# Four interleaved stages after an attention: later key-value products, own orders for the last periods, regrouped activations

## The chip, the cores and the metric

One Trainium2 chip, one core of it. The metric is the device time of one execution in microseconds (us), of which three runs are given and their median is taken. The engines are called PE (matrix products; PEld is its weight load), DVE (vector engine), ACT (scalar engine, for activation functions), POOL (GpSimd) and SP (the engine that issues most transfers).

## The reference, cut to what matters

The input is 4 x 2048 rows of 256 channels. Four sub-layers follow one another, each of the form `x = x + layernorm(sublayer(layernorm(x)))`:

```python
x = x + _layernorm(_L0_attn_ref(_layernorm(x), ...))  # softmax attention, 16 heads of 16
x = x + _layernorm(_L0_ffn_ref(_layernorm(x), ...))   # "f"
x = x + _layernorm(_L1_attn_ref(_layernorm(x), ...))  # "a" and "b"
x = x + _layernorm(_L1_ffn_ref(_layernorm(x), ...))   # "i"

# f: mix every row with the one before it, then
r = sigmoid(xr @ W_r.T); k = relu(xk @ W_k.T) ** 2; out = r * (k @ W_v.T)
# a, b: z = layernorm(x, g1, be1); Q = elu(z @ wq.T) + 1; K = elu(z @ wk.T) + 1; v = z @ wv.T
KV = einsum('nshd,nshv->nhdv', K, v / length)         # over a whole batch of 2048 rows
x = x + Q·KV / (Q·sum(K));  x = x + gelu(layernorm(x, g2, be2) @ w1.T + b1) @ w2.T + b2
# i: weights are integers times 1/127
out = (silu(x @ wg.T) * (x @ wu.T)) @ wd.T
```

Everything is float32.

## The kernel before, in words

The softmax attention comes first (up to about 3,100 us of the span) and writes its result to DRAM tiles `mid`. It is not touched by the change. After it, `rest` treats the other three sub-layers in 16 blocks of 512 rows (four tiles of 128 rows), four blocks to a batch. `narrow` is a flag computed on the chip from the weights; in this execution it is 1, so stage i splits its left operands into a rounded part (`hT`, `gT`) and a remainder (`hL`, `gL`) and makes two fast products of each.

The work of a block is cut into four stages, written as Python generators that yield after each named part:

- `stage_f` (line 155): sums, norm, turn (transposes of `h`, evacuated by ACT into `hT`), mix (ACT scales into `shift`, DVE multiplies and adds into `xk`, `xr`), k0, k1, r, v, osums (statistics of the output on DVE, power on POOL), x (`apply` on DVE, residual on POOL, store to `mid`).
- `stage_a` (line 219): sums, norm, norm2, turn, q0, q1, kv0 to kv3, kv4. Each kv part multiplies one tile for keys and values (one PSUM tile, 128x512), applies `elu1` (DVE minimum, ACT exponential, DVE maximum and sum) to get `K`, and copies the values to `V` on ACT. `gather` then accumulates K^T V into two PSUM tiles over a batch. Part kv_i gathers tile i-1, and kv4 gathers tile 3; in the last block of a batch kv4 also copies the result to `kvm` (16 small DVE copies).
- `stage_b` (line 282): pre (POOL writes the normalised x to `hb`, line 287), msg (Q times `kvm`, DVE divides, POOL adds to `hb`, line 310), sums, norm, turn, up0 to up3 (eight products with GELU on ACT into `hf`), down0 to down3 (DVE adds the bias, POOL adds `hb`, line 332), osums, x.
- `stage_i` (line 341): sums, norm, turn, gate0 to gate5, down0 to down3, osums, x (with the store to `out`). A gate part makes two PSUM tiles; ACT takes SiLU of the first (`gs`), DVE multiplies by the second, ACT rounds to `gT`, POOL makes `gL` (line 382).

A loop over periods p (line 436) steps through these parts in an order written out as a string. In period p, f works on block p, a on block p-2, b on block p-6 and i on block p-7. `next:` and `last:` in the string mean the generator of the following or the preceding period. The order `RAMP` (line 416) serves p = 0 to 5, `FULL` (line 409) all later periods. Since there are 16 blocks, f ends with p = 15, a with p = 17, b with p = 21, i with p = 22 (its last two parts with p = 23).

PE, ACT and DVE instructions of `rest` stay in program order (class `InOrder`, line 38; that is why the profile gives line 46 for nearly all of them). POOL and SP instructions are placed by the scheduler. All matrix products of `rest` share four rotating PSUM tiles `m` (`mm_tile`, line 96), all transposes two tiles `t`; a product waits until the reader of the tile four allocations earlier is done. `hb` has one buffer, `K` two, `V` two (`vs`, line 91), `msg` three, `QT` five.

Of the kernel before, what the change touches and what calls it, by code (L numbers as in the profile page):

```python
# [10 lines left out]
FP = mybir.dt.float32  # L11
# [7 lines left out]
P = 128  # L19
C = 256  # L20
CC = C // P
# [28 lines left out]
def rest(ctx: ExitStack, tc: tile.TileContext, a: dict, out_rows, mids, env: dict, narrow: bool):  # L50
    nc = tc.nc
# [16 lines left out]
    NB = B * NBLK  # L68
    LAG_A, LAG_B, LAG_I = 2, 2 + NBLK, 3 + NBLK
    early = ctx.enter_context(tc.tile_pool(name="early", bufs=3))  # L70
    late = ctx.enter_context(tc.tile_pool(name="late", bufs=3))
    quer = ctx.enter_context(tc.tile_pool(name="quer", bufs=LAG_B - LAG_A + 1))
    small = ctx.enter_context(tc.tile_pool(name="small", bufs=LAG_B - LAG_A + 2))
# [12 lines left out]
    kvms, vs = [], []  # L86
    for r in range(2):
        kvm = one.tile([P, CC, P + 4], FP, tag=f"kvm{r}", name=f"kvm{r}")
        nc.gpsimd.memset(kvm, 0.0)
        kvms.append(kvm)  # L90

        v = one.tile([P, CC, P + 4], FP, tag=f"v{r}", name=f"v{r}")
        nc.gpsimd.memset(v, 1.0 / T)
        vs.append(v)
# [124 lines left out]
    def stage_a(j):  # L219
# [31 lines left out]

        last = None
        for i in range(4):
            kvp = mm_tile()
            linear(kvp, lambda c: zT[:, c, i * P : (i + 1) * P], lambda c: wkv[:, c, :], CC)
            K = two.tile([P, C], FP, tag="K", name="K")
            elu1(K, kvp[:, :C], C)
            V = vs[i % 2]
            act.activation(
                V[:, :, :P],  # L260
                kvp[:, C:].rearrange("p (c d) -> p c d", c=CC),
                AF.Copy,
                scale=1.0 / T,
            )
            if last:
                gather(*last)
            last = i, K, V
            yield f"kv{i}"
        gather(*last)
        if k == NBLK - 1:  # L270
# [11 lines left out]
    def stage_b(j):  # L282
        x, kvm, QT = xs[j], kvms[j // NBLK % 2], queries.pop(j)
        mv, rs = before.pop(j)
        hb = one.tile([P, 4, C], FP, tag="hb", name="hb")
        for i in range(4):
            ln_apply(hb[:, i, :], x[:, i, :], mv, rs, i, nc.gpsimd)
        yield "pre"
        for i in range(4):
# [12 lines left out]
            dve.reciprocal(zr, zr)  # L302
            msg = three.tile([P, C], FP, tag="msg", name="msg")
            dve.tensor_tensor(
# [36 lines left out]
    def stage_i(j):  # L341
# [65 lines left out]


    FULL = (
        "f:turn i:turn b:msg i:gate0 a:turn last:i.osums f:mix i:gate1 b:sums last:i.x load i:gate2 f:k0 "  # L410
# [4 lines left out]
    )  # L415
    RAMP = (
        "load f:turn a:turn f:mix a:q0 next:a.sums a:q1 f:k0 next:a.norm f:k1 a:kv0 next:f.sums a:kv1 "
        "next:a.norm2 a:kv2 next:f.norm a:kv3 f:r a:kv4 f:v f:osums f:x next:b.pre"
    )
# [549 lines left out]
```

## Time and profile before

| | us |
|---|---|
| median of 3 runs | 4578.01 (4574.43 to 4578.36) |
| the profiled execution | 4576.01 |
| its span (first to last instruction) | 4574.2 |
| `rest`, about 3100 to 4574 of the span | 1474 |
| one full period (p = 8 to 15), one is 3592.62 to 3674.50 | 81.88 |
| first i:turn of p = 18 (4272.51) to the end | 301.7 |
| ACT_TABLE_LOAD, 102 of them | 130.9 busy, 1283 ns each |

The span is given in us from its start. In the profile an instruction row has its start, its length, the engine, the line, what it writes and reads, and in brackets the idle time of the engine before it with the instruction that ended that idle time.

### The profile page before, as it was taken

The page shows a single profiled execution, that of the slowest core. Times are in us where ns is not written, and L with a number is a line of the kernel's source. Part 1 is how long each engine was busy: PE and PEld are TensorE (multiplying, and loading weights), DVE is VectorE, ACT ScalarE, POOL GpSimd, SP SyncE. Part 2 cuts the span into 40 slices and gives each one's busy share as a digit, 9 for nine tenths or more (in the row PEclk, how much of TensorE's full clock was granted, in tenths as well). Part 3 has the DMA queues.
Part 4 walks back from the last instruction along what each step waited for, and adds up shares of the span by engine and source line. Part 5 has one row for each costly group of instructions (what it writes and reads, how often), then busy time and mean ns, then how long its engine had stood idle before and what let it go on. Part 6 is the DMA issues. An engine that isn't in the chain of part 4 may idle for free.

```text
span 4574.2 us, 69494 instructions
## 1 busy us (share of the span) xinstructions
PE 4196.7 (92%) x26369; PEld 2196.9 (48%) x26369; DVE 3394.8 (74%) x6847; ACT 2874.5 (63%) x3558; POOL 1089.5 (24%) x1541
## 2 busy tenths in 40 slices
PE   4999999999999999999999999984789899899887
PEld 1444444444444444444444444432456666666665
DVE  4898898988889988889898888954555545554333
ACT  0677777777777777777777777763555555655343
POOL 3100111211001221011121100013234544444344
PEclk9999999999999999999999999997999999999998
DMA  3101101011010020110101101002000000000000
GB/s 107 38 10 29 29 10 42 29 43 36 11 30 23 25 65 10 29 29 10 43 29 31 38 10 29 1 24 72 33 14 28 19 33 24 28 19 19 10 19 15
DMA packets 84568, 130.58 MB, mean 29 GB/s; under 512 B 21376, under 2 KB 41984, under 8 KB 84224
## 3 DMA queue, kind: packets, MB, share of 16 engines
q1 hardware_dynamic: 77920, 122.23, 9.0%
q8 instruction: 210, 3.44, 0.3%
q10 hardware_dynamic: 6304, 3.81, 0.3%
q14 instruction: 134, 1.10, 0.1%
HBM read 33.70 MB, written 25.17 MB: 13 GB/s over the span
## 4 chain that ended last, share of the span: by engine, by line
PE 60%; DVE 21%; ACT 9%; POOL 5%; issue 4%; SPq 1%; DMA 1%; ACTq 0%; POOLq 0%; DVEq 0%
PE acc L46 19%; PE s L46 17%; PE w L46 13%; DVE mx L46 10%; PE m L46 8%; PE t L46 2%; ACT p L46 2%; DVE o L46 2%; ACT h L46 2%; POOL hb L537 2%; ACT L46 1%; DVE gs L46 1%; SPq L662 1%; ACT elu L46 1%; PE ot L46 1%
## 5 line engine op out<-in xcount | busy, mean ns | idle before, releaser
L46 DVE TENSOR_REDUCE mx<-s 128x1 f32<-128x512 f32 x4096 | 2538.8, 682 | 305.0 <-PE s L46 304.9
L46 ACT ACTIVATE p<-w 128x1024 f32<-128x1024 f32 x2048 | 2002.7, 1022 | 824.4 <-PE s L46 556.9
L46 PE MATMUL s<-k,q 64*128 64x512 f32 x4096 | 1664.3, 450 | 56.8 <-DMA k<-lo 30.3
L46 PE MATMUL w<-mrow,pick 64*128 64x512 f32 x4096 | 1406.2, 417 | 0.0
L46 PE MATMUL w<-q,k 64*128 64x512 f32 x4096 | 1369.3, 419 | 0.0
L46 PEld LDWEIGHTS s<-k,q 64*128 64x128 f32 x4096 | 758.5, 186 | 1269.2 <-DVE mx L46 1147.0
L46 PE MATMUL acc<-p,xp 128*32 128x512 f32 x8192 | 1093.3, 605 | 0.0
L46 PEld LDWEIGHTS w<-mrow,pick 64*128 64x128 f32 x4096 | 749.1, 185 | 55.2
L46 PEld LDWEIGHTS w<-q,k 64*128 64x128 f32 x4096 | 670.5, 185 | 58.2 <-ACT p L46 21.7
L627 POOL TENSOR_SCALAR xd<-x,lnx_nm,lnx_rs 128x128 f32<-128x128 f32 x256 | 110.9, 448 | 991.3 <-PE t L46 991.0
L609 POOL TENSOR_SCALAR xp<-x,lnx_nm,lnx_rs 128x64 f32<-128x64 f32 x256 | 99.1, 394 | 921.9 <-PE acc L46 921.0
L46 PEld LDWEIGHTS acc<-p,xp 128*32 128x32 f32 x8192 | 161.6, 108 | 247.0 <-issue 245.8
L46 DVE SCALAR_TENSOR_TENSOR gs<-m,gs 128x512 f32<-128x512 f32 x96 | 66.2, 690 | 226.9 <-ACT gs L46 205.6
L46 PE MATMUL m<-zT,w1T 128*128 128x512 f32 x512 | 225.4, 593 | 0.4 <-ACT zT L46 0.4
L46 PE MATMUL m<-w2T,hf 128*128 128x256 f32 x1024 | 225.6, 379 | 0.0
L46 PEld LDWEIGHTS m<-w2T,hf 128*128 128x128 f32 x1024 | 194.6, 190 | 38.4 <-issue 13.4
L382 POOL TENSOR_TENSOR gL<-gs,gT 128x512 fp32r<-128x512 f32 x96 | 124.4, 1296 | 198.3 <-ACT gT L46 198.2
L46 PE MATMUL t<-ident,h 128*128 128x128 f32 x512 | 90.2, 312 | 88.5 <-ACT h L46 55.9
L46 ACT ACTIVATE elu<-elu 128x256 f32<-128x256 f32 (+1 forms) x96 | 46.7, 487 | 196.4 <-DVE elu L46 196.2
L46 ACT ACT_TABLE_LOAD x102 | 130.9, 1283 | 58.3 <-DVE elu L46 24.6
L46 PEld LDWEIGHTS m<-zT,w1T 128*128 128x128 f32 x512 | 97.4, 190 | 110.6 <-issue 99.3
L140 POOL TENSOR_TENSOR x<-x,o 128x256 f32<-128x256 f32 x192 | 141.8, 767 | 17.9 <-DVE o L46 17.9
(146 smaller groups left out, 4065.4 us busy)
## 6 DMA issues: line engine op xcount, KB each, us to landing
q<-hi SPq DMA_DIRECT2D x256, 64.0 KB, 2.1
k<-hi SPq DMA_DIRECT2D x256, 64.0 KB, 2.1
q<-lo SPq DMA_DIRECT2D x256, 64.0 KB, 2.1
k<-lo SPq DMA_DIRECT2D x256, 64.0 KB, 2.1
mid<-x SPq DMA_DIRECT2D x32, 512.0 KB, 2.6
x<-mid SPq DMA_DIRECT2D x32, 512.0 KB, 3.3
x<-in_x SPq DMA_DIRECT2D x16, 512.0 KB, 5.8
out<-x SPq DMA_DIRECT2D x16, 512.0 KB, 2.9
```

The costliest lines, as they stand in the source:

```text
L46: return lambda *args, **kw: self._tc.keep_in_program_order(method(*args, **kw))
L140: nc.gpsimd.tensor_tensor(x[:, i, :], x[:, i, :], o[:, i, :], ALU.add)
L382: nc.gpsimd.tensor_tensor(gL[:, f, :], gs, gT.bitcast(FP)[:, f, :], ALU.subtract)
L537: dve.tensor_scalar(dst, src, mv[:, i, 0:1], rs[:, i : i + 1], ALU.subtract, ALU.mult)
L609: nc.gpsimd.tensor_scalar(heads(n)[:, i, :, :HD], xs[b][:, i, g * GH * HD : (g + 1) * GH * HD].rearrange("p (h d) -> p h d", d=HD), nm[:, ...
L627: nc.gpsimd.tensor_scalar(xd[:, i], xh.unsqueeze(1).broadcast_to([P, 2, GH * HD]), nm[:, it : it + 1], rs[:, it : it + 1], ALU.add, ALU.mult,)
L662: nc.sync.dma_start(out=dst.bitcast(FP)[r::4, cols], in_=part.bitcast(FP)[c0 : c0 + 32, :])
```

## The change

Gathers come two tiles behind their kv part instead of one, so `K` and `V` get three buffers, and kv4 (now two gathers, and the `kvm` copies) is called in the next period, after f:turn. `hb` gets a second buffer; `msg` and `QT` give one up each. In `FULL`, mix and gate1 come ahead of `last:i.osums`, and all six gate parts come ahead of b:turn (before, gate4 and gate5 were between parts of up). In `RAMP` both q parts come together, the k parts are put between kv parts, and r comes ahead of `next:f.norm`. Two new orders are added: `TURN` for p = 18 and `LATE` for p = 19 to 23. They put i's gates behind b's down, and call the next block's b:msg, b:sums, b:norm and i:turn between and behind them. In the program of the narrow branch the ACT table loads go from 101 to 62 (one more is in the attention).

```diff
-    quer = ctx.enter_context(tc.tile_pool(name="quer", bufs=LAG_B - LAG_A + 1))
+    quer = ctx.enter_context(tc.tile_pool(name="quer", bufs=LAG_B - LAG_A))
...
-    for r in range(2):
-        kvm = one.tile([P, CC, P + 4], FP, tag=f"kvm{r}", name=f"kvm{r}")
-        nc.gpsimd.memset(kvm, 0.0)
-        kvms.append(kvm)
+    for r in range(3):
+        if r < 2:
+            kvm = one.tile([P, CC, P + 4], FP, tag=f"kvm{r}", name=f"kvm{r}")
+            nc.gpsimd.memset(kvm, 0.0)
+            kvms.append(kvm)
...
-        last = None
+        behind = []
         for i in range(4):
             kvp = mm_tile()
             linear(kvp, lambda c: zT[:, c, i * P : (i + 1) * P], lambda c: wkv[:, c, :], CC)
-            K = two.tile([P, C], FP, tag="K", name="K")
+            K = three.tile([P, C], FP, tag="K", name="K")
             elu1(K, kvp[:, :C], C)
-            V = vs[i % 2]
+            V = vs[i % 3]
...
-            if last:
-                gather(*last)
-            last = i, K, V
+            behind.append((i, K, V))
+            if i > 1:
+                gather(*behind.pop(0))
             yield f"kv{i}"
-        gather(*last)
+        for late in behind:
+            gather(*late)
...
-        hb = one.tile([P, 4, C], FP, tag="hb", name="hb")
+        hb = two.tile([P, 4, C], FP, tag="hb", name="hb")
...
-            msg = three.tile([P, C], FP, tag="msg", name="msg")
+            msg = two.tile([P, C], FP, tag="msg", name="msg")
...
     FULL = (
-        "f:turn i:turn b:msg i:gate0 a:turn last:i.osums f:mix i:gate1 b:sums last:i.x load i:gate2 f:k0 "
-        "b:norm i:gate3 f:k1 f:r b:turn i:gate4 b:up0 i:gate5 f:v b:up1 f:osums b:up2 f:x b:up3 "
-        "a:q0 next:f.sums b:down0 a:q1 next:a.sums b:down1 next:f.norm b:down2 next:a.norm b:down3 "
-        "a:kv0 next:b.pre i:down0 b:osums a:kv1 i:down1 b:x a:kv2 next:a.norm2 i:down2 next:i.sums "
-        "a:kv3 i:down3 a:kv4 next:i.norm"
+        "f:turn last:a.kv4 i:turn b:msg i:gate0 a:turn f:mix i:gate1 last:i.osums i:gate2 b:sums "
+        "i:gate3 last:i.x load f:k0 b:norm i:gate4 f:k1 i:gate5 b:turn f:r b:up0 f:v b:up1 f:osums "
+        "b:up2 f:x b:up3 a:q0 next:f.sums b:down0 a:q1 next:a.sums b:down1 next:f.norm b:down2 "
+        "next:a.norm b:down3 a:kv0 next:b.pre i:down0 b:osums a:kv1 i:down1 b:x a:kv2 next:a.norm2 "
+        "i:down2 next:i.sums a:kv3 i:down3 next:i.norm"
     )
     RAMP = (
-        "load f:turn a:turn f:mix a:q0 next:a.sums a:q1 f:k0 next:a.norm f:k1 a:kv0 next:f.sums a:kv1 "
-        "next:a.norm2 a:kv2 next:f.norm a:kv3 f:r a:kv4 f:v f:osums f:x next:b.pre"
+        "load f:turn last:a.kv4 a:turn f:mix a:q0 a:q1 next:a.sums a:kv0 f:k0 next:a.norm a:kv1 f:k1 "
+        "a:kv2 next:f.sums a:kv3 next:a.norm2 f:r next:f.norm f:v f:osums f:x next:b.pre"
     )
+    TURN = (
+        "i:turn last:a.kv4 b:msg i:gate0 last:i.osums b:sums i:gate1 last:i.x load b:norm i:gate2 "
+        "b:turn b:up0 b:up1 b:up2 b:up3 b:down0 next:b.pre b:down1 b:down2 b:down3 b:osums i:gate3 "
+        "next:b.msg i:gate4 b:x next:b.sums i:gate5 next:i.sums i:down0 next:b.norm i:down1 "
+        "next:i.norm i:down2 i:down3 next:i.turn"
+    )
+    LATE = (
+        "b:turn b:up0 b:up1 b:up2 b:up3 b:down0 last:i.osums b:down1 last:i.x load next:b.pre b:down2 "
+        "b:down3 b:osums i:gate0 i:gate1 b:x next:b.msg i:gate2 i:gate3 next:b.sums i:gate4 "
+        "next:i.sums i:gate5 next:b.norm i:down0 i:down1 next:i.norm i:down2 i:down3 next:i.turn"
+    )
...
-        for item in (RAMP if p < LAG_B else FULL).split():
+        order = LATE if p > NB + LAG_A else TURN if p == NB + LAG_A else FULL if p >= LAG_B else RAMP
+        for item in order.split():
```

The scheduler's placement of POOL instructions moves too. In a full period `hb<-x` (line 287 before, four instructions) stood behind the fourth `o<-o,hb` of the same period; now it stands behind the last `gL` and ahead of the statistics of f. In p = 19 and 20 it stands behind the fourth `o<-o,hb` and ahead of b's `lno_rs`.

More of the change, by code (lines that the diff above doesn't have):

```diff
@@ L405, in stage_i @@
         yield "x"
+    RAMP = (
+        "load f:turn last:a.kv4 a:turn f:mix a:q0 a:q1 next:a.sums a:kv0 f:k0 next:a.norm a:kv1 f:k1 "
+        "a:kv2 next:f.sums a:kv3 next:a.norm2 f:r next:f.norm f:v f:osums f:x next:b.pre"
+    )
     FULL = (
-        "f:turn i:turn b:msg i:gate0 a:turn last:i.osums f:mix i:gate1 b:sums last:i.x load i:gate2 f:k0 "
[4 rows of a table removed]
-    )
-    RAMP = (
-        "load f:turn a:turn f:mix a:q0 next:a.sums a:q1 f:k0 next:a.norm f:k1 a:kv0 next:f.sums a:kv1 "
-        "next:a.norm2 a:kv2 next:f.norm a:kv3 f:r a:kv4 f:v f:osums f:x next:b.pre"
+        "f:turn last:a.kv4 i:turn b:msg i:gate0 a:turn f:mix i:gate1 last:i.osums i:gate2 b:sums "
[4 rows of a table added]
+    )
+    TURN = (
[5 more added lines that the diff above has]
+    LATE = (
[3 rows of a table added]
     )
```

## The prediction

> **What bounds the kernel now.** I read the whole-span shares first, then a table of stages, then PE's rows with the idle time before them.
>
> ```profile
> PE 4196.7 (92%) x26369; PEld 2196.9 (48%) x26369; DVE 3394.8 (74%) x6847; ACT 2874.5 (63%) x3558; POOL 1089.5 (24%) x1541
> ```
> ```profile
> core 0: us, PE busy (x) PEld busy (x) DVE busy (x) ACT busy (x) POOL busy (x), PEclk, DMA share, GB/s
> 3100.00:3331.00 231.00, 150.26 (x513) 88.19 (x513) 129.35 (x374) 107.88 (x205) 71.53 (x105) 0.86 0.15 52
> 3428.90:4084.09 655.19, 596.99 (x2560) 412.92 (x2561) 347.01 (x1073) 370.02 (x632) 317.04 (x400) 1.00 0.07 26
> 4084.09:4272.51 188.42, 176.51 (x728) 123.72 (x729) 85.31 (x254) 85.58 (x147) 82.89 (x102) 0.96 0.04 15
> 4272.51:4574.20 301.69, 239.44 (x1000) 176.31 (x1000) 104.94 (x321) 114.39 (x182) 128.13 (x148) 0.88 0.05 17
> ```
>
> The 92% is an average over stages with different limits, and the attention is most of it. The change acts in four stages after it: the ramp (PE busy 65%), eight full periods (91%, PE idle 7.3 us of 81.9 each, granted clock 1.00), p = 16 and 17, and the tail from p = 18 (busy 79%, clock 0.88). Waits are all that can be won: 58 us in the full periods, 62 in the tail, 81 in the ramp. The rows say which.
>
> ```profile
> 3637.98 0.72 PE L46 MATMUL kv<-v,K 128*128 128x132 f32 x4 [1.44 <-ACT v L46]
> 3640.68 1.14 PE L46 MATMUL t<-ident,h 128*128 128x128 f32 x8 [1.11 <-ACT hT L46]
> 3652.08 1.98 PE L46 MATMUL m<-xk,WkT 128*128 128x512 f32 x4 [1.18 <-ACT gs L46]
> 3657.36 1.98 PE L46 MATMUL m<-xk,WkT 128*128 128x512 f32 x4 [1.43 <-DVE gs L46]
> 4339.13 2.80 PE L46 MATMUL t<-ident,h 128*128 128x128 f32 x8 [8.58 <-ACT h L46]
> ```
>
> A full period has eight short waits: 0.25 and 1.44 for values (gathers), 1.11 for i:turn, 0.57 for msg, and 1.18, 1.43, 0.74 and 0.43 for gates. The tail has two long ones a period, 8.58 ahead of i:turn and about 4.18 ahead of b:turn. Behind the 8.58, and behind the value waits, stands one chain on POOL and DVE:
>
> ```profile
> 3624.47 4.85 POOL L537 TENSOR_SCALAR hb<-x,lna_mv,lna_rs 128x256 f32<-128x256 f32 x4
> 3629.29 1.04 POOL L533 TENSOR_TENSOR lno_rs<-lno_ve,neghalf 128x4 f32<-128x4 f32 x1
> ```
> ```profile
> 3630.36 2.23 DVE L46 TENSOR_SCALAR o<-o,lno_mv,lno_rs 128x256 f32<-128x256 f32 x4 [1.42 <-POOL lno_rs L533]
> ```
>
> The 4.85 us of pre hold up the power for b's output; its apply holds up everything behind it on DVE.
>
> **Full periods, p = 7 to 15; kv to msg.** PE runs without a wait from v to down3 before and after, so I follow one period from there, on the clock of the rows above. With pre gone ahead on POOL (second hb buffer), lno_rs can start at 3627.75, when its sums are done, and apply at 3628.94, behind K1: 1.42 earlier. Minimum, exponential, K and V of tile 2, norm2, tile 3, then i.norm follow in ACT's order, each by its own row (0.42, 0.42, 0.42, 0.38, 1.96): i.norm starts at 36.9, not 38.09. PE ends down3 at 35.55, runs f:turn (0.95) and two gathers (0.37 each), and then waits 2.2 for f's `hT` copies, which stand behind i.norm on ACT. The waits of 0.25 + 1.44 + 1.11 become one of 2.2: i:turn at 39.5 instead of 40.68, msg 1.2 earlier.
>
> **The gates.** The order on DVE becomes mix, gs1, osums (2.25), gs2, b:sums (2.25), gs3, apply (2.2), gs4. From msg at 40.5: gate0 at 43.05, mix ends 51.3, gs1 51.3, gs2 54.2, gs3 57.2. PE now has three gates in a row on four `m` tiles, so it waits 1.15 for SiLU 1, 0.25 for gs2 and SiLU 3, 0.8 for gs3, then, since b.norm (2.06) stands ahead of SiLU 4 on ACT, 1.4, and 1.1 for r's first sigmoid (r ends on PE at 67.7; zT, table load, sigmoid at 68.75). That is 4.7 where 1.18 + 1.43 + 0.74 + 0.43 = 3.8 stood. Net per period 1.2 - 0.9 = 0.3 gained, **9 x 0.3 = 2.7 us**. No row shows this order, so its bounds: all eight waits gone gives -7; the two sums (4.5) wholly uncovered and nothing won gives +4.5. I stay near 0, because the same rows with their places changed give it, and carry -2 to +2.5 into the range.
>
> **p = 16, 17.** The same without f: i:turn 1.2 earlier, but zT of b now stands behind gate4's and gate5's round trips on ACT (SiLU 0.60, wait for DVE 0.76, cast 0.62, twice), and nothing of f fills PE: up0 at 62.9 against 62.1, **2 x 0.8 = +1.6**.
>
> **kvm.** The 16 copies (2.18 us, row "COPY kvm<-kv x16") lay under PE's gathers and i:turn. Now they stand behind f's tail copy on DVE, ahead of hL and msg: msg moves from 42.5 to about 44.2. Cover gone, 1.7 in p = 6, 10, 14: **+5.1**.
>
> **Ramp.** A period is 38.4 us, bound by the DVE and ACT chain: shift, mix, table load, elu, sums. With q0 and q1 together, k0 and k1 among the kv parts, and f.norm (2.06) behind r instead of ahead of kv3's exponential, v starts 1.3 earlier (34.3 + 1.3 us after f:turn before, 3277.59 against 3276.3). Four periods give 5.2, and p = 0 and 1, where f.norm alone stood ahead of r, some 1.5 each: **-8**. Kept bounds: 0 and -15.
>
> **Tail.** TURN: kvm is uncovered (3 us until msg), the two sums follow gate0 directly; b:turn at about 4290, down3 ends at 4321.7, three gates with msg and sums between them, the next b:turn at 4343.6. So 71.1 us for p = 18. LATE, counted from b:turn: turn and up0's wait 2.2, up 13.7 and down 13.8 end at 29.7; gate0, gate1 to 33.5; msg to 36.2. Now the hole. pre of the next block needs its x, whose buffer comes free with i.x of the block three earlier. That x is stored and the next one loaded on SP:
>
> ```profile
> 4358.05 0.39 SPq L404 DMA_DIRECT2D out<-x  x1
> 4360.99 0.32 SPq L152 DMA_DIRECT2D x<-mid  x1
> ```
>
> The load issues 2.9 after the store and lands 3.3 later. i.osums stands behind down0, so apply ends at 25.7, the residual on POOL at 26.9, x is there at 33.0, pre runs 33.0 to 37.9, and b's lno_rs stands behind it on POOL (38.9). apply to 41.1, msg0 42.0; gate2 waits 5.8, gate3 1.55 more (msg has two buffers, and POOL's additions stand behind gL and the residual). The last gL ends at 56.7: down0 waits 4.2; the next b:turn at 62.9. PE work 48.2, waits 14.7. Before, such a period took 67.5 and 66.3 (4339.13 to 4406.64 to 4472.99). p = 21 has no next b: from its b:turn to the end 52.3 + 33.6 = 85.9. Sum 71.1 + 2 x 62.9 + 85.9 = 282.8 against 301.7: **-18.9**. If x came in time, b's lno_rs would run at 33.1 and the period would take 57.4: 11 more. If pre were to hold up each of three periods by 5 more: +15.
>
> **Table loads.** 39 fewer, 39 x 1.283 = 50 us of ACT; none ended a PE wait in the full periods except through the chain already followed, so I add nothing for them.
>
> The table load has these rows, the next function starting as it ends:
>
> ```profile
> 3662.79 1.28 ACT L46 ACT_TABLE_LOAD   x1
> 3664.08 1.21 ACT L46 ACTIVATE r<-m 128x256 f32<-128x256 f32 x4
> ```
>
> [...]
>
> After the idle 8.58, eight transposes took 2.80; behind no hole they take 1.04. [...]
>
> **Sum.** -2.7 + 1.6 + 5.1 - 8 - 18.9 = -22.9. The profiled execution took 4576.0 (span 4574.2 and 1.8 around it): 4553.1. It lies 2.0 below the median, so against the median this is the same gain with 4555; I say 4554.
>
> **Rivals.**
>
> *Slower: gates in a row.* ACT handles a gate as SiLU, a wait for DVE's product, cast: 0.60 + 0.76 to 1.1 + 0.62, some 2.0 to 2.3, against 1.87 of PE, and DVE has two sums and an apply among them. If these don't overlap as followed, a full period loses 4 us: 11 x 4 = 44, less the tail, the ramp and the kvm terms (21.8): 4598. For: ACT waited 61 us for gs products in eight full periods already. Against: DVE is busy 53% there. It decides from (22 + 9) / 11 = 2.8 us per period.
>
> *Much faster: the waits go.* If i:turn's and the gates' waits fall to 2 of 7.2 us, 11 x 5 = 55 more is won in place of 1: about 4500. For: PE is the fullest engine; against: ACT's `hT` copies stay behind i.norm.
>
> *Nothing to measure.* pre's wait for x makes p = 19 and 20 as long as before (67.5 + 66.3, 8.0 more than followed), and the ramp is at its bound of 0 (8 more): -6.9, 4569. For: i.x stands late in LATE; against: the followed rows.
>
> **How the numbers follow.** Forecast 0.48 (4530 to 4568), nothing 0.17, slower 0.20, much faster 0.15. A measurement tells some 0.2% (9 us) from no change. Faster is 0.48 + 0.15, same 0.17. Eleven full-order periods at -2 to +2.5 give -20 to +29 around the sum and the tail -11 to +15; taken together 4517 to 4590, which leaves 0.2 out.
>
> **What would show it.** Right: 63 table loads; no gather waits; one wait of about 2 us ahead of i:turn; full periods of 81 to 82; p = 19 and 20 at 63 with a hole of about 6 us that ends in `hb<-x` waiting for x; kvm copies in a wait of p = 10 and 14. Wrong: full periods beyond 84 or below 79, a tail above 300, or pre not waiting for its load.

## The result and the profile after

| | before | changed |
|---|---|---|
| median, us | 4576.25 (4574.43 to 4578.36, 6 runs) | 4595.34 (4594.43 to 4597.15, 6 runs) |
| ratio to before, 95% interval | | 1.0042 [1.0029, 1.0055] |
| span of the profiled execution | 4574.2 | 4595.3 |

The changed kernel is slower, by 19 us of the median and 21.1 of the span. Table loads fell from 102 (130.9 us) to 63 (80.8 us), and no stage shows a gain from that. The same table of stages as before, of the changed kernel, cut at the same instructions: ramp to k of p = 6, eight full periods, then to the first i:turn of p = 18, then the tail.

```profile
core 0: us, PE busy (x) PEld busy (x) DVE busy (x) ACT busy (x) POOL busy (x), PEclk, DMA share, GB/s
3100.00:3337.89 237.89, 158.05 (x513) 96.25 (x513) 126.55 (x374) 107.77 (x204) 76.62 (x110) 0.83 0.14 49
3441.35:4100.67 659.32, 604.13 (x2562) 423.60 (x2561) 347.83 (x1073) 339.36 (x608) 315.68 (x400) 0.98 0.07 25
4100.67:4292.84 192.17, 176.11 (x718) 119.06 (x716) 83.08 (x250) 78.52 (x141) 76.49 (x97) 0.96 0.04 14
4292.84:4595.30 302.46, 241.92 (x1008) 178.69 (x1008) 112.72 (x322) 103.74 (x174) 127.33 (x148) 0.90 0.05 16
```

231.00 became 237.89, 655.19 became 659.32, 188.42 became 192.17, and the tail, from which nearly all was expected, stayed (301.69 and 302.46). In the tail PE was idle 62.3 us before and 60.5 now, and busy 239.4 and 241.9. Cut at f's product v, which every period has once, the ledger is:

| from, to | before | changed | difference | predicted |
|---|---|---|---|---|
| start to v of p = 5 | 3316.41 | 3316.05 | -0.4 | -8 |
| v of p = 5 to v of p = 7 | 110.09 | 122.90 | +12.8 | +1.4 |
| v of p = 7 to v of p = 15 | 655.19 | 659.32 | +4.1 | +1.0 |
| v of p = 15 to i:turn of p = 18 | 190.82 | 194.57 | +3.7 | +1.6 |
| i:turn of p = 18 to the end | 301.69 | 302.46 | +0.8 | -18.9 |

The forecast was a gain of 22.9 us and the result, between the profiled executions, a loss of 21.1. Of the 44.0 between them, 19.7 lie in the tail, 11.4 in p = 6 and 7, 7.6 in the ramp, and 3.1 and 2.1 in the rows between.

Below, "a period" runs from v to v, and from p = 16 on, where f has no v, from b's down0 to the next. The plain full periods of the changed kernel take 81.57 us (81.87 before); p = 10 and 14, the first of a batch, take 84.82 and 84.09.

The largest loss is in p = 6. Rows of the changed kernel's timeline (start, length, engine, what it does, idle time before it with the instruction that ended it):

```profile
3326.01 2.19 DVE L46 TENSOR_SCALAR o<-o,lno_mv,lno_rs 128x256 f32<-128x256 f32 x4 [1.16 <-POOL lno_rs L548]
3328.79 2.17 DVE L46 COPY kvm<-kv 32x32 f32<-32x32 f32 x16
3329.91 0.81 PE L46 MATMUL m<-kvm,QT 128*128 128x132 f32 x2 [6.15 <-DVE kvm L46]
3334.90 1.45 ACT L46 ACTIVATE zT<-t,be,g 128x512 f32<-128x512 f32 x2 [11.36 <-PE t L46]
3336.99 1.41 DVE L46 SCALAR_TENSOR_TENSOR xk<-hT,mu_k,shift 128x512 f32<-128x512 f32 x2 [1.59 <-ACT shift L46]
```

The `kvm` copies stand on DVE behind f's apply of the period before. PE waits 6.15 for them with b:msg, a:turn is behind b:msg on PE, ACT waits 11.36 for a:turn, and f's `shift` and `xk` are behind that. So one late group of copies holds up three engines in turn.

The tail, p = 19, same columns:

```profile
4404.85 4.85 POOL L552 TENSOR_SCALAR hb<-x,lna_mv,lna_rs 128x256 f32<-128x256 f32 x4 [2.61 <-DMA x<-mid]
4409.66 1.03 POOL L548 TENSOR_TENSOR lno_rs<-lno_ve,neghalf 128x4 f32<-128x4 f32 x1
4410.73 3.73 DVE L46 TENSOR_SCALAR o<-o,lno_mv,lno_rs 128x256 f32<-128x256 f32 x4 [4.27 <-POOL lno_rs L548]
4415.38 0.76 PE L46 MATMUL m<-hT,wgT 128*128 128x512 f32 x1 [8.14 <-DVE zr L46]
```

The foreseen hole is there (pre waits for its load, the power stands behind pre, apply behind the power, msg behind apply), but it is 8.14 us, not 5.8. LATE's periods took 66.55 and 67.61, not 62.9. Yet PE's waits in them were no longer than forecast. The rows below run from b:turn of p = 19 to b:turn of p = 20 in the changed kernel, and from i:turn of p = 19 to i:turn of p = 20 before; both hold the same products.

```profile
4371.57:4438.18 66.61, 53.43 (x225) 39.68 (x225) 24.88 (x69) 22.84 (x38) 29.03 (x34) 0.90 0.05 16
```
```profile
4339.13:4406.64 67.51, 54.57 (x225) 39.63 (x225) 21.99 (x68) 25.59 (x41) 29.31 (x34) 0.88 0.05 16
```

Of 66.61 us PE was busy 53.43 and idle 13.18, at a granted clock (column PEclk, the share of full speed that PE was given) of 0.90. The forecast had 48.2 and 14.7.

### The profile page after: what moved, and what is told of

It reads as the page before. It is cut to its first block, busy times and chain, and to the rows that moved or that the text cites. A ratio compares the mean times of both kernels' runs of the same rounds, so it can differ in the third digit from the quotient of the medians.

```text
span 4595.3 us, 69548 instructions
## 1 busy us (share of the span) xinstructions
PE 4215.9 (92%) x26369; PEld 2216.9 (48%) x26369; DVE 3398.1 (74%) x6847; ACT 2824.5 (61%) x3519; POOL 1086.9 (24%) x1542
## 4 chain that ended last, share of the span: by engine, by line
PE 66%; DVE 18%; ACT 7%; issue 4%; POOL 3%; DMA 1%; SPq 1%; ACTq 0%; DVEq 0%; POOLq 0%
PE acc L46 19%; PE s L46 17%; PE m L46 15%; PE w L46 13%; DVE mx L46 10%; PE t L46 2%; ACT p L46 2%; ACT h L46 1%; DVE gs L46 1%; DVE lno_st L46 1%; DVE o L46 1%; ACT zT L46 1%; SPq L677 1%; ACT L46 1%; PE ot L46 1%
## 5 line engine op out<-in xcount | busy, mean ns | idle before, releaser
L46 ACT ACTIVATE hf<-m,b 128x512 f32<-128x512 f32 x128 | 87.9, 687 | 156.6 <-PE m L46 156.1
L46 ACT ACT_TABLE_LOAD x63 | 80.8, 1283 | 145.5 <-PE m L46 102.3
L46 DVE TENSOR_TENSOR o<-m,r 128x256 f32<-128x256 f32 x64 | 27.2, 424 | 158.4 <-PE m L46 115.1
```

The costliest lines, as they stand in the source:

```text
L46: return lambda *args, **kw: self._tc.keep_in_program_order(method(*args, **kw))
```

## The experiments

All labels below name runs; times are medians, ratios are to the kernel before in the same session, and positions come from each run's profiled execution. "Expected" is quoted as it stood before the run.

**kv4 at home (e1).** Both last gathers and the `kvm` copies back at the end of their own period (`last:a.kv4` goes from `FULL` and `TURN` as well).

```diff
-        "load f:turn last:a.kv4 a:turn f:mix a:q0 a:q1 next:a.sums a:kv0 f:k0 next:a.norm a:kv1 f:k1 "
-        "a:kv2 next:f.sums a:kv3 next:a.norm2 f:r next:f.norm f:v f:osums f:x next:b.pre"
+        "load f:turn a:turn f:mix a:q0 a:q1 next:a.sums a:kv0 f:k0 next:a.norm a:kv1 f:k1 "
+        "a:kv2 next:f.sums a:kv3 next:a.norm2 f:r next:f.norm a:kv4 f:v f:osums f:x next:b.pre"
...
-        "i:down2 next:i.sums a:kv3 i:down3 next:i.norm"
+        "i:down2 next:i.sums a:kv3 i:down3 a:kv4 next:i.norm"
```

> Both gathers of kv4 and the 16 kvm copies go back to the end of their own period, in the ramp, the full periods and the turn; all else as in the changed kernel. In the changed kernel the time from v of p = 5 to v of p = 6 is 40.0 us (29.5 before), and p = 10 and 14 are 84.8 and 84.1 (other full periods 81.6). Theory A (the copies, once they stand behind f's last apply and the tail copies on DVE, hold up b:msg and all that follows it on PE and ACT): 40.0 falls to about 30, p = 10 and 14 to about 82; full periods grow by the gather waits that come back, 0 to 0.8 each (0 to +6 over eight). Sum -15 to -8 us against the changed kernel's 4595. Rival B (the loss at p = 6 is the ramp's new order and its lower clock, which end in p = 6): 40.0 stays above 37, sum -5 to +3.

4572.6, ratio 0.9987 [0.9977, 0.9996]: 22.7 less than the changed kernel. v to v over p = 6 fell from 40.0 to 32.8, p = 10 and 14 to 81.6 both, and the other full periods stayed at 81.60. In the ramp v of p = 5 came 4.2 earlier. The start of p = 6 in this run:

```profile
3310.18 2.15 DVE L46 COPY kvm<-kv 32x32 f32<-32x32 f32 x16 [2.62 <-PE kv L46]
3318.45 1.97 PE L46 MATMUL m<-kvm,QT 128*128 128x132 f32 x16
3320.89 1.45 ACT L46 ACTIVATE zT<-t,be,g 128x512 f32<-128x512 f32 x2 [1.60 <-PE t L46]
```

The copies fill a gap in which DVE waited anyway, msg waits for nothing, and ACT's wait for a:turn falls from 11.36 to 1.60. Theory A holds in its mechanism; its size was too small (-15 to -8), since the ramp won 4.2 too and the stretch behind v of p = 15 another 5. kv4's move wins nothing in a full period. The 32.8 still holds a slow v of p = 5 (5.91 us, granted clock 0.62); where that v took 3.69, as in e5 to e8 and e10, p = 6 took 30.6.

**The ramp's order of before (e2).** The rest as in the changed kernel, but p = 6 leaves out `last:a.kv4`, which p = 5 has done.

```diff
-        "load f:turn last:a.kv4 a:turn f:mix a:q0 a:q1 next:a.sums a:kv0 f:k0 next:a.norm a:kv1 f:k1 "
-        "a:kv2 next:f.sums a:kv3 next:a.norm2 f:r next:f.norm f:v f:osums f:x next:b.pre"
+        "load f:turn a:turn f:mix a:q0 next:a.sums a:q1 f:k0 next:a.norm f:k1 a:kv0 next:f.sums a:kv1 "
+        "next:a.norm2 a:kv2 next:f.norm a:kv3 f:r a:kv4 f:v f:osums f:x next:b.pre"
```

> The ramp's order of before, with kv4 in its own period up to p = 5; from p = 6 on as in the changed kernel (kv4 a period late). In the changed kernel the first query product stands 4.9 us earlier than before at p = 2, 1.7 at p = 3, 0.3 later at p = 4, 1.0 later at p = 5 and 10.2 later at p = 6. Theory A (kv4 at the start of p = 6 costs some 10 us, the ramp's new order gained 5 in its first periods and lost them by p = 5): p = 2 to 5 within 1.5 us of before, p = 6 within 1.5 of before as well, since kv4 of p = 5 is at home; sum about -10 against the changed kernel. Rival B (the full order's first period is what costs, whatever stands ahead of it): p = 6 still 8 or more later, sum -3 to +1. If p = 2 to 5 are gained by over 2 us against before, the new ramp order did harm and not nothing.

4594.6, 1.0035 [1.0023, 1.0048]. The sum, -0.8, is where B had it, but not for B's reason, and A's instants are missed too: v of p = 5 already came 8.1 later than before. Of that 3.1 came between v of p = 0 and v of p = 1, where the order is the same and v of p = 0 was slow (6.75 us at a granted clock of 0.54, 3.69 before). In p = 3 to 5 it was 0.9 to 1.3 each: two gathers stood between r and v there (1.97 us in p = 4 at a granted clock of 0.50, 0.61 for the one of before). p = 6 took 31.4 from v to v, so the loss there goes with kv4's place; the ramp was left for e13.

**x of late blocks into a free buffer (e3).**

```diff
-                    load(p + 1 - LAG_B, late)
+                    load(p + 1 - LAG_B, early if p > NB + LAG_A else late)
```

> From p = 19 on the next block's x is loaded into one of the buffers of f's and a's x, which are free by then, in place of the buffer that the store of block three earlier must leave; all else as in the changed kernel. There a full wait of 8.1 us stood on PE in p = 19 and 20 between gate1 and gate2, and the normalised x waited 2.6 for its load. Theory A (the late load holds up the pre stage, and the power for b's output behind it on POOL): the wait falls to 2 to 4, p = 19 and 20 go from 66.5 and 67.6 to 59 to 62, sum -9 to -13 against the changed kernel. Rival B (what counts is the 4.85 us that pre takes on POOL ahead of the power, wherever its load lands, and the slower work on DVE beside it): only the 2.6 goes, 64 to 65 a period, sum -4 to -6.

4590.1, 1.0027 [1.0017, 1.0036]. p = 19 went to 64.7, as B had it, with 5.60 of PE's wait left; p = 20 to 61.1, as A had it. The load's wait is gone, pre's 4.85 ahead of the power is not.

**b:turn ahead of gate4 and gate5 in p = 16 and 17 (e4).**

```diff
+    MID = (
+        "last:a.kv4 i:turn b:msg i:gate0 a:turn last:i.osums i:gate1 b:sums last:i.x load i:gate2 "
+        "b:norm i:gate3 b:turn i:gate4 b:up0 i:gate5 b:up1 b:up2 b:up3 "
...
```

> For p = 16 and 17 alone b:turn goes back ahead of gate4 and gate5, which stand between parts of up again, as before; all else as in the changed kernel, where these periods take 74.1 and 74.2 us (71.6 before). Theory A (with nothing of f to fill in, b:turn waits for its copies behind two gates' round trips on ACT): both fall to 71 to 72, sum -4 to -6. Rival B (the two sums on DVE that come ahead of gs2 and gs3, or the gathers at the start, take the time): 73.5 to 74.5, sum -1 to +1.

4590.9, 1.0028 [1.0018, 1.0038]; the periods fell from 74.1 and 74.2 to 70.7 and 71.2 (p = 18 gave 1.8 back). Theory A. What it cost is seen in the changed kernel's p = 16:

```profile
4167.89 0.59 ACT L46 ACTIVATE gs<-m 128x512 f32<-128x512 f32 x1
4169.30 0.62 ACT L46 CAST gT<-gs 128x512 fp32r<-128x512 f32 x1 [0.81 <-DVE gs L46]
4169.82 1.44 ACT L46 ACTIVATE zT<-t,be,g 128x512 f32<-128x512 f32 x2
4170.65 2.07 PE L46 MATMUL m<-zT,w1T 128*128 128x512 f32 x2 [3.70 <-ACT zT L46]
```

zT stands behind a gate's SiLU, DVE's product and the cast, and PE has nothing else: 3.70 us.

**The three together (e5)**, the edits of e1, e3 and e4.

> Three of the edits together: kv4 at home in its own period, b:turn ahead of gate4 and gate5 in p = 16 and 17, and x of the late blocks loaded into a free buffer. Alone they changed the changed kernel's 4595 by -22.7, -4.5 and -5.2 us. If the three sit in different places of the span (p = 2 to 15 and 18; 16 and 17; 19 and 20) they add: 4563, between 4558 and 4567. Rival: they share one slack (a shorter p = 17 only lengthens p = 18, as in the run with b:turn moved, where p = 18 took 71.7 in place of 70.0): 4568 to 4573.

4560.1, 0.9962 [0.9948, 0.9976]: they add.

**The old order from p = 18 on (e6)**, with kv4 at home and e4's order for p = 16 and 17; x is loaded as in the changed kernel.

```diff
-        order = LATE if p > NB + LAG_A else TURN if p == NB + LAG_A else MID if p >= NB else FULL if p >= LAG_B else RAMP
+        order = OLD if p >= NB + LAG_A else MID if p >= NB else FULL if p >= LAG_B else RAMP
```

> kv4 at home, b:turn ahead of the last gates in p = 16 and 17, and from p = 18 on the order of before in place of TURN and LATE. Theory A (TURN and LATE as they stand won nothing: 301.7 us from the first i:turn of p = 18 to the end before, 301.0 changed): within 3 us of the sum of the first two edits, 4568, and 301 to 303 from p = 18's first i:turn to the end. Rival B (the tail's orders do gain some 5 us a period in p = 19 to 21, and kvm and the old start of p = 18 hid it): 4573 or more.

4560.2, 0.9963 [0.9949, 0.9977]. Better than either theory: from p = 18's first msg to the end 289.7 us, where the kernel before took 299.6 with the same order. (The 301.0 in the expectation counts from the fourth transpose of i:turn; from the first it is 302.5.) The wait ahead of i:turn was 5.28 in place of 8.58. The buffers, which had been priced only through the new orders, seemed to do something to the old one; e9 tries them alone.

**pre called first in LATE (e7)**, on e5.

```diff
-        "b:turn b:up0 b:up1 b:up2 b:up3 b:down0 last:i.osums b:down1 last:i.x load next:b.pre b:down2 "
+        "load next:b.pre b:turn b:up0 b:up1 b:up2 b:up3 b:down0 last:i.osums b:down1 last:i.x b:down2 "
```

> As the three edits together, with the load of the next block's x and its pre stage called at the head of LATE, so that POOL's 4.85 us run while PE is at up, and the power for b's output is not behind them. Theory A (in p = 19 the 5.6 us wait left on PE between gate1 and gate2 is those 4.85 us ahead of the power): p = 19 falls from 64.7 to 60 to 61, p = 20 stays at about 61 or falls by 2; -3 to -6 us against the three edits. Rival B (the wait comes from the apply on DVE, which takes 3.7 us there in place of 2.2 beside POOL's work, and from the residual): the wait stays above 4, -2 to 0.

4560.3, 0.9962 [0.9948, 0.9976], no change. It decides nothing: POOL's place is the scheduler's, and it left pre behind the fourth `o<-o,hb`, ahead of the power, so PE still waited 5.64.

**Gathers one tile behind again (e8)**, on e1, with the new orders.

```diff
-            if i > 1:
+            if i > 0:
```

> kv4 at home as in that run, and the gathers one tile behind their kv part again, as before; the orders stay the new ones. With two behind and kv4 at home a full period took 81.60 us (81.57 with kv4 a period late, 81.87 before). Theory A (the two tiles of distance win the gather waits of 0.25 and 1.44, and that is the 0.27 gained): full periods go to 81.9 or more, +2 to +8 us over nine periods against 4572.6. Rival B (the 0.27 comes from pre's earlier place and the gates' order; the gather waits are only moved): full periods stay within 0.1 of 81.60, and the ramp's periods, where one gather instead of two stands ahead of v, get 0.4 to 1 shorter: -4 to 0.

4575.1, 0.9995 [0.9985, 1.0005]. Full periods 81.60: the distance of two wins nothing there (B). The ramp's periods p = 3 to 5 got 0.2, 0.8 and 2.1 longer, against B's expectation, and the whole is 2.5 longer, as A had it, but not in the full periods.

**The buffers alone (e9)**: the kernel before with nothing but

```diff
-    quer = ctx.enter_context(tc.tile_pool(name="quer", bufs=LAG_B - LAG_A + 1))
+    quer = ctx.enter_context(tc.tile_pool(name="quer", bufs=LAG_B - LAG_A))
...
-        hb = one.tile([P, 4, C], FP, tag="hb", name="hb")
+        hb = two.tile([P, 4, C], FP, tag="hb", name="hb")
...
-            msg = three.tile([P, C], FP, tag="msg", name="msg")
+            msg = two.tile([P, C], FP, tag="msg", name="msg")
```

> The kernel before with the changed kernel's buffers for hb, msg and QT alone (hb two, msg two, QT four); all orders and the gathers as before. Theory A (of the whole change it is the second hb buffer that wins: it lets POOL's 4.85 us of pre go ahead, out of the way of the power for b's output): in p = 19 and 20 the wait ahead of i:turn falls from 8.58 to about 5.3 as in the run with the old tail, so the tail gains about 3.3 each in p = 18 to 20, and full periods fall from 81.87 to 81.6 or below; 4577 - 10 - 3 = 4564, between 4560 and 4569. Rival B (pre goes ahead only because the new orders call other work around it): within 3 us of 4577.

4552.1, 0.9948 [0.9932, 0.9965]: 24.7 us less than before, twice what theory A had. `hb` is the only one of the three that grew. Full periods fell to 80.33 and the tail from the first msg to 290.6. The tail of this run, p = 19 and the start of p = 20:

```profile
4344.70 4.85 POOL L537 TENSOR_SCALAR hb<-x,lna_mv,lna_rs 128x256 f32<-128x256 f32 x4 [3.19 <-DMA x<-mid]
4374.88 1.04 POOL L533 TENSOR_TENSOR lno_rs<-lno_ve,neghalf 128x4 f32<-128x4 f32 x1 [1.60 <-DVE lno_ve L46]
4382.90 2.80 PE L46 MATMUL t<-ident,h 128*128 128x128 f32 x8 [5.30 <-ACT h L46]
```

pre runs 30 us ahead of the power, which now waits only for its own sums; PE's 8.58 is 5.30. The full period's two gather waits (0.25 and 1.44 before) are one of 0.42.

**msg ahead of b:x in LATE (e10)**, on e7.

```diff
-        "b:down3 b:osums i:gate0 i:gate1 b:x next:b.msg i:gate2 i:gate3 next:b.sums i:gate4 "
+        "b:down3 b:osums i:gate0 i:gate1 next:b.msg b:x i:gate2 i:gate3 next:b.sums i:gate4 "
```

> As the run with pre called at the head of LATE, and in LATE the next block's b:msg called ahead of b:x. There PE waits 5.6 us in p = 19 and 20 between gate1 and gate2, on DVE's first step of msg, which stands behind b's apply (3.7 us) and so behind POOL's power and pre. Theory A (that place in DVE's order is what the wait is made of): it falls below 2, and p = 19 and 20 get 3 to 5 shorter each, less what gates then wait for msg's two buffers and for apply: -4 to -9 us against 4560. Rival B (apply and the residual come later by the same amount and hold up i's output chain instead): 0 to +4.

4556.1, 0.9956 [0.9939, 0.9973]. The 5.64 fell to 1.63, with 1.78 new behind it: DVE's order made the hole, and 2.2 us of it came back in p = 19 (64.6 to 62.4), none in p = 20 (61.1 and 61.0). From p = 18's first msg to the end e10 takes 288.7 us.

**The old full order in p = 6 and 7 (e12)**, on e6.

```diff
-        order = OLD if p >= NB + LAG_A else MID if p >= NB else FULL if p >= LAG_B else RAMP
+        order = OLD if p >= NB + LAG_A or LAG_B <= p <= LAG_I else MID if p >= NB else FULL if p >= LAG_B else RAMP
```

> As the run with kv4 at home, b:turn ahead and the old tail, and with the old full order in p = 6 and 7 as well, where stage i has no or little work. There v of p = 5 to v of p = 6 took 30.6 and the next period 82.9 (29.5 and 80.6 before). Theory A (the new full order, with gates before turn and mix ahead, costs in the periods where i has nothing to fill in): 29.5 and 80.7, -3 us against 4560. Rival B (it is the gathers two behind, whose two waits at the end of p = 6 take 6.6 us in place of 6.7 in four, and the hand-over between orders): within 1 us.

4558.1, 0.9958 [0.9942, 0.9975]. p = 6 to 8 took 31.8, 81.6 and 82.4 (30.6, 82.9 and 81.6 in e6): mostly shifted; the 2.1 of the medians lies within their intervals.

**The new ramp with kv4 at home, on the buffers alone (e13)**, gathers two behind in the first batch only.

```diff
-            if last:
-                gather(*last)
-            last = i, K, V
+            behind.append((i, K, V))
+            if i > (1 if j < NBLK else 0):
+                gather(*behind.pop(0))
```

and e1's `RAMP`, K and V in three buffers.

> The run with the buffers alone (4552, orders of before), with the new ramp order and gathers two behind added for the first batch only, kv4 at home. Theory A (the new ramp order does win what was forecast, some 8 us, and only kv4's move into the next period took it back): v of p = 5 goes from 3316 to 3309 and the whole to 4545, between 4542 and 4548. Rival B (the ramp's gain was the clock's luck in the runs that showed it): within 3 us of 4552.

4553.9, 0.9951 [0.9937, 0.9964]. v of p = 5 came at 3307.6, 8.3 before e9's 3316.0: the ramp won what was forecast. The whole lies where B had it, but because the full periods rose from 80.33 to 81.37, with the orders of before and the gathers one behind. Ahead of v in p = 5, first the changed kernel, then this run:

```profile
3312.30 1.13 PE L46 MATMUL m<-WrT,xr 128*128 128x256 f32 x4 [2.04 <-ACT v L46]
3316.05 5.94 PE L46 MATMUL m<-WvT,ka 128*128 128x256 f32 x16 [2.61 <-ACT r L46]
```
```profile
3303.89 1.13 PE L46 MATMUL m<-WrT,xr 128*128 128x256 f32 x4 [2.05 <-ACT v L46]
3304.86 1.06 PE L46 MATMUL kv<-v,K 128*128 128x132 f32 x8
3307.64 3.69 PE L46 MATMUL m<-WvT,ka 128*128 128x256 f32 x16 [1.72 <-ACT r L46]
```

At home the gathers fill part of the wait for r's sigmoid. Taken away, PE is idle 0.9 longer, and v behind it takes 5.94 in place of 3.69, at a granted clock of 0.62 in place of 1.00. The other runs agree: in the four kernels with the new ramp and kv4 a period late (the changed one, e3, e4, e16) all 16 v of p = 2 to 5 took 5.2 to 6.7; in the nine with kv4 at home and the same ramp (e1, e5, e6, e7, e10, e12, e13, e17, e19) 31 of 36 took 3.7. v of p = 5 came at 3316.0 to 3316.9 in the four and at 3307.6 to 3311.8 in the nine.

**Two halves of the full order (e14, e15)**, each on e9.

```diff
-        "b:norm i:gate3 f:k1 f:r b:turn i:gate4 b:up0 i:gate5 f:v b:up1 f:osums b:up2 f:x b:up3 "
+        "b:norm i:gate3 i:gate4 f:k1 i:gate5 b:turn f:r b:up0 f:v b:up1 f:osums b:up2 f:x b:up3 "
```

> The run with the buffers alone (full period 80.34 us), with gate4 and gate5 called ahead of b:turn and r behind it, as in the changed kernel; mix and gate1 stay behind the output sums. The changed kernel's order takes 81.60 with the same buffers, 1.26 more. Theory A (that loss is b:turn's copy and r's sigmoid standing behind two gates' round trips on ACT, 1.31 us of which show as a wait for r ahead of the first up): 81.1 to 81.6, and p = 16 and 17 lose 2 to 3 us each: +10 to +16 against 4552. Rival B (it is the sums that come between the gates' products on DVE): 80.3 to 80.6 and 0 to +7 from p = 16 on.

```diff
-        "f:turn i:turn b:msg i:gate0 a:turn last:i.osums f:mix i:gate1 b:sums last:i.x load i:gate2 f:k0 "
-        "b:norm i:gate3 f:k1 f:r b:turn i:gate4 b:up0 i:gate5 f:v b:up1 f:osums b:up2 f:x b:up3 "
+        "f:turn i:turn b:msg i:gate0 a:turn f:mix i:gate1 last:i.osums i:gate2 b:sums i:gate3 last:i.x load f:k0 "
+        "b:norm f:k1 f:r b:turn i:gate4 b:up0 i:gate5 f:v b:up1 f:osums b:up2 f:x b:up3 "
```

> The run with the buffers alone (full period 80.34 us), with mix and gate1 ahead of the output sums and gate3 up to b:sums, as in the changed kernel; from k on the order of before. Theory A of the run with gate4 and gate5 ahead (the loss of 1.26 sits there): this one stays at 80.0 to 80.6. Rival B (three gates in a row with two sums among their products, a wait of 1.96 to 2.15 us ahead of gate3's products where 1.17 and 1.42 stood ahead of k): 81.1 to 81.6, +8 to +14 against 4552.

4557.9, 0.9960 [0.9944, 0.9975], and 4561.5, 0.9968 [0.9956, 0.9979]. Full periods 80.68 and 80.20: +0.35 and -0.13. Neither is the 1.24 between 80.33 and 81.57, so neither theory has the place. (e15's loss is in p = 16 and 17, 73.4 and 72.2, where nothing of f stands among the gates.)

**The place of a table load (e16).** In e13's and e9's full periods PE and DVE agree up to the first gate; on ACT the table load of the first SiLU stands elsewhere. The program's own list of ACT's waits:

```
e9:    table load                      SiLU gs<-m, waits for PE
e13:   table load, waits for PE        SiLU gs<-m, waits for ACT
```

In the traces the changed kernel, e1, e6, e8 and e13, all with three buffers for K and V, have the load behind the wait and periods of 81.4 to 81.6; e9, e14 and e15, with two, have it ahead of the wait and 80.2 to 80.7 (so has the kernel before, at 81.87 with its one `hb`). e16 is the changed kernel plus

```diff
+        act.activation(one.tile([P, 1], FP, tag="warm", name="warm"), b1[:, :1], AF.Silu)
         for f in range(NHID):
```

> The changed kernel with one small SiLU (128x1) added on ACT ahead of each block's first gate. In the traces the table load of the first SiLU stands without a wait and ends before the product is there in the kernel before and in the runs whose period is 80.2 to 80.7 (50.7, SiLU at 53.7 after a wait for PE of 1.66), and in all runs whose period is 81.4 to 81.6 it is itself what waits for PE (2.98) and then takes 1.28 in front of the SiLU. Theory A (this place of the table load is the lost 1.0 to 1.3 us a period): with the small SiLU the load runs early; full periods fall from 81.57 to 80.2 to 80.7, p = 16 and 17 by about 1; -9 to -14 us against the changed kernel's 4595. Rival B (the gates' waits are set by DVE and the order, and the load is absorbed): full periods stay above 81.3, -3 to +1.

4583.9, 1.0015 [1.0005, 1.0024]: 11.5 less than the changed kernel, full periods 80.63. ACT's rows at i:turn and gate0, the changed kernel and then e16:

```profile
3569.43 1.07 ACT L46 CAST hT<-t 128x512 fp32r<-128x512 f32 x2 [0.26 <-PE t L46]
3573.49 1.28 ACT L46 ACT_TABLE_LOAD   x1 [2.99 <-PE m L46]
3574.78 0.60 ACT L46 ACTIVATE gs<-m 128x512 f32<-128x512 f32 x1
```
```profile
3567.95 1.07 ACT L46 CAST hT<-t 128x512 fp32r<-128x512 f32 x2 [0.26 <-PE t L46]
3569.04 1.28 ACT L46 ACT_TABLE_LOAD   x1
3570.34 0.20 ACT L46 ACTIVATE warm<-b 128x1 f32<-128x1 f32 x1
3572.03 0.60 ACT L46 ACTIVATE gs<-m 128x512 f32<-128x512 f32 x1 [1.49 <-PE m L46]
```

From cast to SiLU it is 5.35 in the one and 4.08 in the other: the load, 1.28, waits for the gate's product in the first and runs during that wait in the second.

**The best version (e17, e18)**: e13 with e16's SiLU; e18 with a small exponential ahead of a's first query product as well.

```diff
         queries[j] = QT = quer.tile([P, CC, IB], FP, tag="QT", name="QT")
+        act.activation(one.tile([P, 1], FP, tag="warm", name="warm"), b1[:, :1], AF.Exp)
```

> The run with the buffers, the new ramp and kv4 at home (4554, period 81.38), with the same small SiLU. Theory A: period 80.3 as with the buffers alone, the ramp's 8 us kept: 4554 - 9 x 1.05 - 1 each for p = 16 and 17 = 4542, between 4539 and 4546. Rival B: within 3 us of 4554.

> As the run before, with a small exponential (128x1) added on ACT ahead of a's first query product as well. In the ramp the exponential's table load waits 1.80 for DVE's minimum and then takes 1.28 in front of the exponential, on the DVE and ACT chain that sets a ramp period. Theory A: ramp periods p = 2 to 5 go from 38.0 and 37.6 to some 36.5, and p = 6 too: -4 to -6 us against the run before. Rival B (the keys' and v's chain, not the queries', ends last in the ramp): -1 to +1.

e17: 4540.2, 0.9919 [0.9905, 0.9932], inside theory A's 4539 to 4546. It beats both kernels, the one before by 37 us. Its table of stages:

```profile
core 0: us, PE busy (x) PEld busy (x) DVE busy (x) ACT busy (x) POOL busy (x), PEclk, DMA share, GB/s
3100.00:3323.20 223.20, 150.81 (x513) 91.02 (x513) 126.25 (x374) 108.29 (x205) 76.95 (x110) 0.85 0.15 53
3421.28:4064.81 643.53, 594.41 (x2561) 413.67 (x2561) 345.47 (x1073) 371.79 (x640) 316.12 (x400) 1.00 0.08 26
4064.81:4249.93 185.12, 174.72 (x728) 121.35 (x728) 84.50 (x254) 85.95 (x149) 77.89 (x98) 0.97 0.04 15
4249.93:4541.20 291.27, 240.38 (x1000) 178.40 (x1000) 104.65 (x321) 115.37 (x187) 127.64 (x148) 0.89 0.05 17
```

Every stage is shorter than in both kernels. Eight periods take 643.5 us beside 659.3 in the changed kernel, with 32 us more of ACT work (371.79 and 339.36), since the old orders keep their table loads. e18: 4541.1, 0.9922 [0.9909, 0.9936], no difference that can be told. Its ramp periods fell to 36.6 to 36.8 as A had it (4.8 earlier at v of p = 5), and p = 6 gave 2.2 back.

**TURN and LATE on the best version (e19)**, the changed kernel's strings without `last:a.kv4`, and its choice of orders.

```diff
-        for item in (RAMP if p < LAG_B else FULL).split():
+        order = LATE if p > NB + LAG_A else TURN if p == NB + LAG_A else FULL if p >= LAG_B else RAMP
+        for item in order.split():
```

> The best version so far (buffers, new ramp with kv4 at home, small SiLU, 4540) with TURN and LATE of the changed kernel from p = 18 on in place of the old order. From p = 18's first msg to the end the best version takes 289.2 us (299.6 before). Theory A (with the second hb buffer in both, the new tail orders are worse than the old one, since pre stands ahead of the power for b's output in them and not in the old one): 294 to 299, +5 to +9 us against 4540. Rival B (they are as good, and what the changed kernel lost was kvm and the late start of p = 18): within 2 us of 4540. Rival C (they win, as was forecast): 4536 or less.

4550.5, 0.9943 [0.9930, 0.9957], 10.3 above e17 (6.3 between the profiled executions). From the first msg of p = 18 to the end 295.9 in place of 289.2. The loss is A's: with the same buffers the new tail orders, as they stand, are worse. PE waits 8.23 and 8.31 ahead of gate2 in p = 19 and 20, behind pre and the power; that these waits are the whole loss is not isolated. With x loaded into a free buffer and msg ahead of b:x (e10, 288.7), the new orders are level with the old one on two `hb` buffers.

## Why the prediction was wrong

- **Tail, -18.9: the step that failed most is the price of PE's work, which had no term for the low clock.** The tail was put at 282.8 us and took 302.5. Of the 19.7 missing, 8.4 are in LATE's two periods (66.6 and 67.6 from b:turn to b:turn, for 62.9), 7.6 in p = 18 (78.7 for 71.1) and 3.6 from b:turn of p = 21 on (89.5 for 85.9). LATE's 62.9 was the sum "PE work 48.2, waits 14.7". The waits were 13.2 and 13.1; the work was 53.4 and 54.5. In the kernel before, the same work took 54.6 and 53.2 in the periods of 67.5 and 66.3, with 12.9 and 13.2 idle. So the 8.0 us of gain forecast for p = 19 and 20 came from setting work priced near the full clock against periods measured at granted clocks of 0.88 and 0.91; in waits, "all that can be won", no gain was forecast there. An estimate, each busy stretch of PE weighted by its granted clock: the low clock took 3.6 and 4.7 us of PE's work in LATE's periods (5.2 and 3.8 before) and 20.6 in the whole tail (22.4 before). No run changes the clock alone, so how much of that is on the path is not shown.
- **The hole in LATE.** LATE's chain was there link by link, with a hole of 8.14 for 5.8, of which 1.5 is apply (3.73 us in place of 2.2); the waits behind it were shorter than followed. The first ten products behind the hole ran at a granted clock of 0.50 (0.63 us each in place of 0.39), and the sum has no term for that, though the rows of before gave a like case: the eight transposes in 2.80 us behind the idle 8.58, at a granted clock of 0.50, and in 1.04 behind no hole.
- **The tail's comparison.** The new orders were set against a tail with one `hb`. With two, the old order's periods of p = 19 to 21 fall by 1.6 to 3.1 us of themselves (8.58 to 5.30 ahead of i:turn; 64.4 to 64.8 in e9, 66.3 to 67.7 before), and it keeps pre clear of the power, which LATE does not; from p = 18 on TURN and LATE are 6.7 us worse than it (e19).
- **kvm, 1.7 in each of three periods: mis-sized.** It is 7.2 in p = 6, 3.2 in p = 10 and 2.5 in p = 14 (e1). The working added the copies' length to msg. It left out that DVE's queue ahead of them holds f's apply in p = 6, and that a:turn on PE, zT and shift on ACT and xk on DVE all stand behind msg. The other 5.2 us that p = 6 and 7 lost stay in e1; 2.2 of them go with the slow v of p = 5, and with the order of before as well 0.2 are left (e17, 110.3).
- **Ramp, -8: the term is right for the order and wrong for the change.** e13 shows -8.3 with kv4 at home, though divided otherwise: 4.9 by v of p = 1 and 3.4 in the four periods, for 3 and 5.2. The working did not follow the two gathers that go from ahead of v, where PE waited anyway, to ahead of a:turn, where it did not; v then ran at granted clocks of 0.55 to 0.71.
- **"39 fewer, ... I add nothing": a step that failed in the full periods.** The number of table loads was right and their sum was rightly not counted (e16, with 63 loads, has full periods of 80.63; e17, with 102, of 80.40). Their place was taken as unchanged. Before, the load ahead of the first SiLU lay in a wait of ACT; in the changed kernel it waits first. One load behind a wait cost about 1 us a period, 11.5 in all.
- **Full periods, 0.3 each: the number was right, in part by luck.** The waits came near those followed (1.83 for 2.2 ahead of i:turn; 1.96 + 0.59 + 0.76 + 1.31 = 4.6 for 4.7 at the gates), but what they are made of was not seen. The buffers that let pre go ahead win 1.54 by themselves (e9). Of that the changed kernel gives back 0.94 at the first SiLU (e16), and the remaining 0.30 stands with its order.
- **p = 16 and 17, +0.8 each: the mechanism named, the size a third.** +2.5 and +2.6; e4 takes 3.4 and 3.0 back. The 0.8 was the difference of two instants, with no term for the 3.70 in which PE has no other work.
- **The rivals and signs.** "Gates in a row" gave 4598, close to the result, by a loss of 4 us in each of eleven periods; the plain ones were 0.3 faster, so the number is chance. pre's wait for x, from "nothing to measure", was there (e3). A rival that was missing: the parts of the change pulling against each other, buffers -25, kv4 a period late +23, load behind a wait +11. They were measured on different bases and are not a sum. Of the signs of being wrong a tail above 300 came, and p = 10 and 14 passed 84. The 4517 to 4590 does not follow from the bounds beside it: added to 4554, -20 and -11 give 4523, and +29 and +15 give 4598.

Open: why the SiLU gets a second wait with three K buffers. It goes with the buffers in the runs seen. In the programs of e9 and e13 the second wait is for ACT's own exponential of the second key tile, whose `tmp` buffer `gs` takes over, and which is done by then (in e13 it ends at 3619.55, 15.5 us ahead of the table load at 3635.03); why the program with two K buffers does without that wait was not followed.

## What to carry to other kernels

Price each buffer by itself on the old orders before pricing the orders that were written around it: here the `hb` buffer alone won 24.7 us, and the change as a whole lost 19. Price a new order's work at the clock that the stage had when it was measured (here 1.00 in the full periods before and 0.88 in the tail), or compare waits with waits. Count a table load by where it stands, ahead of or behind the wait for its data, not by number; a tiny activation of the same function ahead of the wait fixed the place here (e16: 11.5 us less than the changed kernel; e17: 13.7 less than e13). When a step moves out of a gap, look for what filled that gap and for what is queued on every engine behind the step's new place.

## What the runs showed of the hardware

- In the changed kernel DVE's apply (four 128x256) took 1.37 us in the 11 cases in which POOL ran little but small pieces beside it, 2.19 to 2.21 in the 30 in which it ran the residual, 2.71 in the three with b's `o<-o,hb` besides, and 2.80 to 3.73 in the four with `gL`. What makes apply longer beside POOL's work is not shown.
- The same 16 products of v took 3.69 us behind a wait of 3.03 (p = 0 before, granted clock 1.00), 5.94 behind 2.61 (p = 5 changed, 0.62) and 5.92 behind 1.27 (p = 5 in e12). In these cases the length of the last wait alone does not tell whether the clock falls. What does is not shown: no run here isolates it.
